# Seven loads of table rows issued as two DMAs each, by rows

## The chip, the cores and the metric

The kernel runs on one core of a Trainium2 chip (trn2). Its time is the device time of one execution, in microseconds (us); the figure for a kernel is the median of its runs. The profile is of one execution, by the hardware profiler, and its times count from the first instruction of the program. Engines: PE (matmuls), PEld (weight loads of PE), DVE (VectorE), ACT (ScalarE), POOL (GpSimd), SP (SyncE, which here only issues DMAs). A core has 16 DMA engines, and every DMA, whichever engine issues it, is carried out by some of these 16.

## The reference

The inputs are a list of 50 items for each of 1024 users, the lists' lengths, and a table of 100001 rows of 128 numbers (f32), whose row 0 counts as zero. What is computed, cut to the core:

```
e = emb[seq]                                  # 1024 x 50 x 128
uF = cumsum(e, axis=1) / min(t, lengths)      # running mean over the items
y = (uF - mean) * rsqrt(var + eps) * gamma + beta   # statistics over the 1024 users, for each t
v = v + (x - v) / 2; spike = v >= 1; v = v - spike  # scanned over the 50 steps
uF_out = mean of the spikes over the steps    # 1024 x 128
scores = uF_out @ emb.T                       # 1024 x 100001, f32
```

The output alone is 409.6 MB, and the table 51.2 MB.

## The kernel before, in words

**First stage** (to about 507 us, when the first store of scores is issued). For each of the 50 steps, rows of the table are gathered (POOL, L204, and 512 single-row DMAs on SP, L197), turned and summed on PE, normalised and compared on DVE and ACT, and spikes are counted. Meanwhile the first 36 blocks of the table (a block is 1024 rows) are loaded by SP into six tiles `rows0` to `rows5`.

**Second stage.** The table has 98 blocks `q`, the last one of 673 rows. A block lies in SBUF as 128 partitions of 1024 numbers, partition p holding rows 8p to 8p+7 of the block, 4 KB in one piece. Each block is prepared once: PE turns it (`turned`, L119), ACT copies the rounded part (`hi`, L141), DVE the rest (`lo`, L142). The 98 blocks are taken in 21 groups of `WIDTHS` blocks: first 2 or 3 at a time, then twelve groups of 6, then two of 4. For each group and each of the eight sets of 128 users (`n`), PE multiplies (`product`, L149) the counts with every block of the group, DVE and ACT in turn copy the result scaled by 1/50 into a tile `o` (L471, L473), and SP stores the tile (`store`, L158): 128 partitions of 24 KB where the group has 6 blocks, 3 MB a store. In the wide groups there are three tiles `o`, used in turn, so the copies for a store wait until the store three places back has landed.

**The loads of the change.** In the wide groups the remaining 62 blocks are loaded while the stores run: after `n` = 1 and `n` = 4 of a group, `fetch` is called for half a group, three blocks. Its DMA (L97) has 128 partitions, three blocks, and 4 KB in each, 1.5 MB, and is issued by ACT, in ACT's program order between its copies, since SP's queue is that of the stores. There are 20 such loads (q = 36, 39, ... 93); then one of a single block (q = 96) and two for the last block: 640 rows as 128 partitions of five pieces of 512 bytes (L106), and 33 rows as 33 partitions of 512 bytes (L111).

**What sets the order.** The order is written out by hand (`manual_schedule`): each engine does its instructions in the order in which the program records them. The completions of the DMAs of SP and ACT are counted by eight semaphores, DMAHW0 to DMAHW7, given out in turn, in program order, to stores and loads alike. A DMA that takes a semaphore waits on its issuing engine until the DMA eight places back, which had the same semaphore, has landed, unless that engine has waited for that already. A store on SP may so wait for a load of ACT.

Of the kernel before, what the change touches and what calls it, by code (L numbers as in the profile page):

```python
# [20 lines left out]
P = 128  # L21
BN_EPS = 1e-5
V_TH = 1.0
HALF = 1024
KQ = HALF // P
# [3 lines left out]

WIDTHS = [2, 2, 2, 3, 3, 3, 3] + 12 * [6] + [4, 4]  # L30
NARROW, MIDDLE = 3, 7


@with_exitstack
def rec_kernel(
# [44 lines left out]
    def size(q):  # L80
        return min(HALF, N - q * HALF)

    def group(g):
        at = g if g < AHEAD else AHEAD - 2 + g % 2
        r = rowp.tile([P, GROUP, HALF], F32, tag=f"rows{at}", name=f"rows_{g}")
        for k in range(GROUP):
            rows[g * GROUP + k] = r[:, k, :]
        return r

    def fetch(r, q, n):  # L90

        engine = nc.sync if q < AHEAD * GROUP else nc.scalar
        k = q % GROUP
        n = min(n, parts - q)
        whole = n - (size(q + n - 1) < HALF)
        if whole:
            engine.dma_start(  # L97
                out=r[:, k : k + whole, :],
                in_=table[q * HALF : (q + whole) * HALF, :].rearrange("(q p k) d -> p q (k d)", p=P, k=KQ),
            )  # L100
        if whole < n:
            full, rest = divmod(size(parts - 1), P)
            c1 = (parts - 1) * HALF
            r = r[:, k + whole, :].rearrange("p (k d) -> p k d", d=D)
            if full:
                engine.dma_start(  # L106
                    out=r[:, :full, :],
                    in_=table[c1 : c1 + full * P, :].rearrange("(k p) d -> p k d", p=P),
                )
            if rest:  # L110
                engine.dma_start(out=r[:rest, full, :], in_=table[c1 + full * P : N, :])  # L111
# [49 lines left out]
    with ExitStack() as ph:  # L161
# [17 lines left out]
        for g in range(AHEAD):  # L179
            fetch(group(g), g * GROUP, GROUP)  # L180
# [113 lines left out]
        whole = slice(0, B)  # L294
# [5 lines left out]
        for t in range(T):  # L300
# [35 lines left out]
            r = sp.tile([P, 1], F32, tag="r", name=f"r_{t}")  # L336
# [10 lines left out]
            q = sp.tile([P, 1], F32, tag="q", name=f"q_{t}")  # L347
# [13 lines left out]
            if not last:  # L361
# [9 lines left out]
                if t in (T - 8, T - 6):  # L371
                    q = (t - T + 8) // 2
# [54 lines left out]
    for c, W in enumerate(WIDTHS):  # L427
# [30 lines left out]
        for n in range(NB):  # L458
# [26 lines left out]
            if n in (1, 4) and c >= MIDDLE and to_fetch < parts:  # L485
                g = to_fetch // GROUP
                if to_fetch % GROUP or to_split >= (g - 1) * GROUP:
                    if to_fetch % GROUP == 0:
                        r = group(g)
                    fetch(r, to_fetch, GROUP // 2)  # L490
                    to_fetch += GROUP // 2
# [21 lines left out]
```

## Time and profile before

| what | value |
|---|---|
| median of 3 runs | 1779.58 us |
| lowest and highest | 1778.25 and 1783.5 us |
| span of the profiled execution, first to last instruction | 1569.9 us |
| the profiled execution's own time | not told by the page |
| median less span (work around the program) | 209.7 us |
| first store of scores issued, last one issued | 506.8 us, 1557.7 us |
| first and last of the three-block loads issued by ACT | 751.7 us, 1383.9 us |
| DMA engines, mean busy share, 700 to 1425 us | 1.00, at 424 GB/s |
| PE, DVE, ACT busy, 700 to 1425 us | 604, 388, 324 of 725 us |

The busy share of the DMA engines is a mean over 16, so it does not tell one engine from another. Two other records of the trace do. Each DMA engine that carries a part of a DMA adds one mark to the DMA's semaphore when its own part has landed, so a store has sixteen marks with a time each, and the store counts as landed at the sixteenth. And every packet that a DMA engine moves has a start, a duration, a size and a queue (q1 for SP's DMAs, q10 for ACT's), though no engine number.

### The profile page before, as it was taken

What the parts mean: (1) busy time and instruction counts of PE and PEld (TensorE: products, weight loads), DVE (VectorE), ACT (ScalarE), POOL (GpSimd) and SP (SyncE); (2) the same over time, 40 slices, a digit from 0 to 9 for tenths busy, and PEclk for the clock granted to TensorE, in tenths of its full rate; (3) what the DMA queues carried; (4) which work ended last, traced back from release to release, by engine and by line L of the source; (5) the groups of instructions that cost most, each with busy time, mean ns of one, the idle gap of its engine ahead of it and who ended that gap; (6) DMA issues with size and microseconds to landing.
All of it is one profiled execution on the core that took longest, in us unless ns stands there. A gap on an engine that the chain in (4) does not pass through costs nothing.

```text
span 1569.9 us, 14231 instructions
## 1 busy us (share of the span) xinstructions
PE 1153.1 (73%) x4548; PEld 822.3 (52%) x4548; DVE 940.7 (60%) x1161; ACT 630.6 (40%) x700; POOL 374.6 (24%) x402
## 2 busy tenths in 40 slices
PE   4555555555556988899878788887788888788784
PEld 2222222222233766677666666666666666666563
DVE  4777777777778665576545555555555545555453
ACT  2322222222233554465444444444444444444342
POOL 6777777777775000000000000000000000000000
PEclk7555555555555999999999988999999998989998
DMA  9622222222222999999999999999999999999998
GB/s 342 245 55 53 55 54 54 54 53 54 52 53 64 399 411 420 420 393 428 425 432 427 429 428 424 418 422 424 428 413 420 415 424 429 421 423 409 394 423 354
DMA packets 54600, 488.25 MB, mean 311 GB/s; under 512 B 12443, under 2 KB 13756, under 8 KB 33276
## 3 DMA queue, kind: packets, MB, share of 16 engines
q1 hardware_dynamic: 33008, 429.03, 65.1%
q0 software_dynamic: 12672, 25.98, 6.2%
q10 hardware_dynamic: 8844, 32.33, 5.2%
q8 instruction: 36, 0.59, 0.1%
q14 instruction: 40, 0.33, 0.1%
HBM read 77.69 MB, written 409.60 MB: 310 GB/s over the span
## 4 chain that ended last, share of the span: by engine, by line
DMA 52%; POOL 17%; PE 11%; issue 9%; ACT 5%; DVE 4%; DVEq 0%; ACTq 0%; SPq 0%; POOLq 0%
DMA scores<-o 49%; POOL e L204 17%; PE po L149 9%; ACT o L473 5%; DMA e<-in_L_rec_emb_table,idx 3%; DVE o L471 2%; PE pt L119 1%; DVE bs L323 1%; DVE uF L322 0%; DVE s L343 0%; PE pre L313 0%; PE sums L281 0%; DMA idx<-in_r_seq 0%; ACT hi L141 0%; ACT pairs L141 0%
## 5 line engine op out<-in xcount | busy, mean ns | idle before, releaser
L471 DVE TENSOR_SCALAR o<-po 128x1024 f32<-128x1024 f32 x391 | 463.5, 1220 | 351.8 <-DMA scores<-o 323.4
L473 ACT ACTIVATE o<-po 128x1024 f32<-128x1024 f32 (+1 forms) x391 | 387.9, 1018 | 547.8 <-DMA scores<-o 344.9
L204 POOL DMA_INDIRECT e<-in_L_rec_emb_table,idx x396 | 373.9, 944 | 123.4 <-issue 114.6
L149 PE MATMUL po<-pairs,countB 128*128 128x512 f32 x1168 | 314.7, 415 | 67.6 <-ACT o L473 50.7
L149 PEld LDWEIGHTS po<-pairs,countB 128*128 128x128 f32 x1168 | 225.8, 198 | 132.5 <-ACT o L473 65.8
L149 PE MATMUL po<-pairs,countC 128*128 128x512 f32 x876 | 239.1, 419 | 43.6 <-ACT o L473 43.6
L313 PE MATMUL pre<-ident,e 128*128 128x128 f32 x396 | 153.1, 450 | 143.8 <-DMA e<-in_L_rec_emb_table,idx 142.2
L149 PEld LDWEIGHTS po<-pairs,countC 128*128 128x128 f32 x876 | 170.1, 200 | 89.7 <-ACT o L473 54.7
L313 PEld LDWEIGHTS pre<-ident,e 128*128 128x128 f32 x396 | 78.5, 201 | 236.1 <-DMA e<-in_L_rec_emb_table,idx 214.7
L142 DVE TENSOR_TENSOR pairs<-pt,pairs 128x1024 fp32r<-128x1024 f32 (+1 forms) x73 | 88.3, 1217 | 96.6 <-ACT pairs L141 96.5
L337 ACT ACTIVATE r<-mv,eps 128x1 f32<-128x1 f32 x50 | 14.7, 295 | 300.6 <-DVE mv L333 300.6
L322 DVE SCALAR_TENSOR_TENSOR uF<-rlen,pre 128x512 f32<-128x512 f32 x100 | 68.3, 683 | 103.8 <-PE pre L313 103.8
L119 PE MATMUL pt<-ident,rows 128*128 128x128 f32 x782 | 113.5, 293 | 8.0 <-ACT o L473 3.9
L119 PEld LDWEIGHTS pt<-ident,rows 128*128 128x128 f32 x782 | 102.6, 154 | 28.8 <-issue 10.0
L149 PE MATMUL po<-hi,countB 128*128 128x512 f32 x200 | 82.8, 414 | 18.8 <-ACT o L473 13.8
L281 PE MATMUL sums<-s,ident_h 128*128 128x512 bf16 x98 | 49.6, 608 | 60.6 <-DVE s L343 60.6
L270 PE MATMUL pre<-zT,l 128*128 128x512 f32 x100 | 78.0, 782 | 21.6 <-DVE uF L322 21.5
L149 PE MATMUL po<-lo,countB 128*128 128x512 f32 x200 | 80.4, 402 | 0.0
L141 ACT CAST pairs<-pt 128x1024 fp32r<-128x1024 f32 (+1 forms) x73 | 73.6, 1008 | 16.2 <-PE pt L119 15.9
L149 PE MATMUL po<-pairs,countA 128*128 128x512 f32 (+1 forms) x292 | 73.2, 393 | 9.1 <-ACT o L473 9.1
L149 PE MATMUL po<-hi,countC 128*128 128x512 f32 x150 | 62.7, 418 | 16.4 <-ACT o L473 16.4
L356 ACT ACTIVATE v<-uF,hgb,a 128x1024 f32<-128x1024 f32 x49 | 59.2, 1208 | 37.4 <-DVE a L352 37.4
(78 smaller groups left out, 821.1 us busy)
## 6 DMA issues: line engine op xcount, KB each, us to landing
scores<-o SPq DMA_DIRECT2D x96, 3072.0 KB
scores<-o SPq DMA_DIRECT2D x32, 1536.0 KB
rows<-in_L_rec_emb_table ACTq DMA_DIRECT2D x20, 1536.0 KB
scores<-o SPq DMA_DIRECT2D x22, 1024.0 KB
rows<-in_L_rec_emb_table SPq DMA_DIRECT2D x6, 3072.0 KB
scores<-o SPq DMA_DIRECT2D x8, 2048.0 KB
scores<-o SPq DMA_DIRECT2D x8, 1872.5 KB
aside<-in_L_rec_emb_table SPq DMA_DIRECT2D x512, 0.5 KB
```

The costliest lines, as they stand in the source:

```text
L119: nc.tensor.transpose(pt[:, k0 : k0 + kw], r[:kw, k0 : k0 + D], ident[:kw, :kw])
L141: nc.scalar.copy(vh, vp)
L142: nc.vector.tensor_tensor(vl, vp, vh.bitcast(F32), ALU.subtract)
L149: nc.tensor.matmul(po[:, :kw], lhsT=counts[n], rhs=part[:, k0 : k0 + kw], start=j == 0, stop=j == 1,)
L204: nc.gpsimd.indirect_dma_start(out=es[t][:, n * P : (n + 1) * P], out_offset=None, in_=table, in_offset=bass.IndirectOffsetOnAxis(ap=idx[: ...
L270: nc.tensor.matmul(pre[h], lhsT=l, rhs=zT[:, h * BANK : (h + 1) * BANK], start=t == 0, stop=False, skip_group_check=True,)
L281: nc.tensor.matmul(sums[h], lhsT=ident_h, rhs=s[:, h * BANK : (h + 1) * BANK], start=t == 0, stop=t == T - 2, skip_group_check=True,)
L313: nc.tensor.matmul(pre[h][:, k : k + P], lhsT=aside[t] if h == k == 0 and t in aside else e[:, h * BANK + k : h * BANK + k + P], rhs=ident ...
L322: nc.vector.scalar_tensor_tensor(uF[:, cs], rlen[:, cs], 1.0 / (t + 1), pre[h], ALU.max, ALU.mult)
L356: nc.scalar.activation(vt, uF[:, cs], AF.Identity, bias=hgb[:, 1:2], scale=a)
L471: nc.vector.tensor_scalar_mul(o[:, h0 : h0 + hw], po[:, :hw], 1.0 / T)
L473: nc.scalar.mul(o[:, h0 : h0 + hw], po[:, :hw], 1.0 / T)
```

## The change

A table `CUTS` names seven of the 20 loads by their first block and gives a number of rows (partitions). Such a load is issued as two DMAs one right after the other, both by ACT into the same tile: the first has that number of partitions, the second has those left, all three blocks in both. All other loads stay as they were, and so does every other instruction. The bytes moved are the same.

```
+CUTS = {39: 120, 48: 126, 57: 104, 66: 108, 75: 88, 84: 120, 90: 120}
...
         if whole:
-            engine.dma_start(
-                out=r[:, k : k + whole, :],
-                in_=table[q * HALF : (q + whole) * HALF, :].rearrange("(q p k) d -> p q (k d)", p=P, k=KQ),
-            )
+            to = r[:, k : k + whole, :]
+            of = table[q * HALF : (q + whole) * HALF, :].rearrange("(q p k) d -> p q (k d)", p=P, k=KQ)
+            cut = CUTS.get(q, P)
+            engine.dma_start(out=to[:cut], in_=of[:cut])
+            if cut < P:
+                engine.dma_start(out=to[cut:], in_=of[cut:])
```

The second pieces have 8, 2, 24, 20, 40, 8 and 8 rows. As the semaphores are given out in turn, each added DMA moves all later DMAs one semaphore on. ACT has seven more instructions; four of them (q = 48, 66, 84, 90) begin with a wait for a semaphore that an earlier load has.

## The prediction

> **What bounds the kernel now.** I read the page first, for where the time lies, then the sums by stretch, the chain and SP's waits, and last the single packets and completion marks.
>
> The page, with the chain that ended last and two groups:
>
> ```profile
> span 1569.9 us, 14231 instructions
> ...
> q1 hardware_dynamic: 33008, 429.03, 65.1%
> ...
> q10 hardware_dynamic: 8844, 32.33, 5.2%
> ...
> DMA 52%; POOL 17%; PE 11%; issue 9%; ACT 5%; DVE 4%; DVEq 0%; ACTq 0%; SPq 0%; POOLq 0%
> ...
> L471 DVE TENSOR_SCALAR o<-po 128x1024 f32<-128x1024 f32 x391 | 463.5, 1220 | 351.8 <-DMA scores<-o 323.4
> L473 ACT ACTIVATE o<-po 128x1024 f32<-128x1024 f32 (+1 forms) x391 | 387.9, 1018 | 547.8 <-DMA scores<-o 344.9
> ```
>
> Stores carry half the chain, and both copying engines stand idle for them. The sums by stretch (us; busy times with counts; granted clock, DMA share, GB/s):
>
> ```profile
> 750.00:1000.00 250.00, 208.32 (x904) 164.39 (x902) 130.90 (x111) 109.96 (x112) 0.00 (x0) 0.92 1.01 426
> 1000.00:1425.00 425.00, 350.13 (x1506) 275.47 (x1507) 225.36 (x191) 186.83 (x190) 0.00 (x0) 0.93 1.00 421
> 1425.00:1475.00 50.00, 42.88 (x191) 33.56 (x190) 26.30 (x23) 22.45 (x23) 0.00 (x0) 0.97 0.95 394
> 1475.00:1563.00 88.00, 63.75 (x272) 49.31 (x270) 42.24 (x38) 32.48 (x36) 0.00 (x0) 0.95 1.00 422
> 1563.00:1570.00 7.00, 0.00 (x0) 0.00 (x0) 0.00 (x0) 0.00 (x0) 0.00 (x0) 0.50 0.08 34
> ```
>
> The DMA engines are full. Summing the packets, the mean engine idles 2.0 us from 750 to 1425, 3.1 us to 1475, 0.1 us to 1563 and 6.2 us after. So the question is not the mean, but which engine ends last. The chain's end (start, us, what):
>
> ```profile
> 1529.53 11.77 DMA scores<-o
> 1541.30 0.03 issue
> ...
> 1542.56 1.23 DVE o L471
> 1543.79 0.02 SPq L158
> 1543.81 0.03 issue
> 1543.84 11.33 DMA scores<-o
> ```
>
> A store takes 11.3 us to its last mark, though the last store's marks come at 1563.5 (the first), 1565.1, 1565.6 and 1568.8: one engine is 5.3 us behind the first. Packets tell which kind of engine. On one engine each packet starts 3 to 4 ns before the last one's end, so they can be threaded into sixteen sequences. Fifteen move a 24 KB store packet in 912 ns (median); one, which I call L, takes 931 to 936. It lags 2 us at 716, 8 us at 925, 7 to 10 us until 1420, and in the stretches that I threaded (1006 to 1563) it has no gap that is more than a packet. L's load packets (4 KB) take 163 ns in the mean, the others' 159. Three other engines lag 2 to 5 us.
>
> **How rows fall to engines.** A DMA of 128 rows leaves 16 marks, 8 rows to an engine; the one of 33 rows leaves 11, three rows each; the single-row ones use one engine. Each is the largest number up to 16 that divides the rows. So I take 120 rows on 15 engines, 126 on 14, 104 on 13, 108 on 12, 88 on 11, and second pieces of 8, 2, 24, 20, 40 rows on 8, 2, 12, 10, 10. If smaller sets lie inside larger ones, the seven loads give the engine in place 0, 1, ... 15: 70, 70, 69 (six times), 66, 66, 60, 52, 41, 33, 24 and 0 rows; before, each has 7 x 8 = 56.
>
> L has a place: it is among the eleven of the 33-row load. Its store packet of 1470.861 is followed at 1471.794 by a 512-byte q10 packet, after it had closed the 640-row load at 1470.855; L alone still had a store then. So L is in places 0 to 10, and gets 4 to 14 rows more.
>
> **The change part by part.**
> 1. *L's rows.* Eight of the eleven places get 13 or 14 rows, so I take 13. A row is three packets: 13 x 3 x 0.163 = 6.4 us; ends 4 x 3 x 0.163 = 2.0 and 14 x 3 x 0.163 = 6.8. Nothing hides it: L has no gap, and the copies wait for L's mark. **+6.4 us.**
> 2. *Relief of places 11 to 15* (4 to 56 rows less, up to 27 us at 0.159 a packet): these engines do not end last, and the stores wait for all sixteen. 0 here; rival A says when not.
> 3. *Seven more issues on ACT.* Rows:
>
> ```profile
> L97 ACTq DMA_DIRECT2D rows<-in_L_rec_emb_table x21: 347/375/417, 751.7 to 1424.9; - x21
> L106 ACTq DMA_DIRECT2D rows<-in_L_rec_emb_table x1: 1272/1272/1272, 1425.3 to 1425.3; - x1
> L111 ACTq DMA_DIRECT2D rows<-in_L_rec_emb_table x1: 1705/1705/1705, 1426.6 to 1426.6; - x1
> ```
>
>    Between 7 x 0.375 = 2.6 and 7 x 1.7 = 12 us of ACT, at seven places. The copies (L473) and the PE products behind them come that much later once, and SP's store with them. ACT idles 272 us for stores from 750 on, and L has a backlog of about 8 us, against 1.7 at most. 0; without that cover, up to 12.
> 4. *Four new waits on ACT* (second pieces of q = 48, 66, 84, 90, each for the load before). Those landed 12.5, 10.5, 8.6 and 9.1 us before the issue times of before. 0. Behind such a wait stand ACT's copies and SP's stores.
> 5. *Semaphores one on.* Stores now wait for loads one store sooner: ten such waits shrink from 11 to 15 us of margin to 2.2 to 8.0 (load 3.7, 2.8, 3.2, 2.2 us for q = 39, 48, 57, 66). Still margins: 0, and L's backlog is behind it. Rival B prices the other case.
> 6. *Later landing of the second pieces*: 40 rows on ten engines are 12 more packets, between store packets of 0.912: 12 x 1.07 = 13 us. PE turns a block 42 to 48 us after its load has landed. 0.
>
> The unchanged tail keeps its own stall, SP's wait for the 640-row load:
>
> ```profile
> SPq L158 <- DMA rows<-in_L_rec_emb_table: 13.9, 1, 13.9
> ```
>
> Sum: +6.4, so a span of 1576.3 and, against the median, 1779.6 + 6.4 = **1786.0 us**. The page doesn't tell the profiled execution's own time; I take the 209.7 us around the span as unchanged.
>
> [...] The trace has L in the eleven, which speaks against the change. No trace here shows engine numbers.
>
> **The rivals.**
> - *A, the relieved engines are the ones that bind (faster).* If the sets do not nest and L is outside most of them, L loses up to 56 rows and stops binding. Then the ten or so loaded engines bind: they ended 5.3 us earlier, had about 2 us of gaps, and get 6.2 us (13 x 3 x 0.159): -1. At best all gaps but the 3.1 us of the tail's stall go: -8. Middle -4: 1775.6. For: the relief is steep, and two of the three smaller laggards are outside the eleven. Against: L's packets at 1471. It decides as soon as L carries under 56 rows.
> - *B, a wait opens.* If load marks come 8 us later (L's backlog), the ten margins turn into about 33 us of waiting on SP. The 13.9 us of the tail cost the mean engine 3.1 us; at that rate 33 cost 7.4: 1786.0 + 7.4 = 1793.4. Decides when a load lands over 3 us later.
> - *C, packets of narrower DMAs are slower.* The gathers' 4 KB packets average 244 ns. L's 207 load packets at 244 instead of 163: +16.8, so 1802.8. Against: the 33-row load's packets took 27 ns like the 640-row load's.
> - *D, hidden.* L sits at place 10, or gains from emptier neighbours (its store packets take 912 at best): +1, 1780.6.
>
> **How the numbers follow.** Chances: forecast 0.50, A 0.26, D 0.12, B 0.08, C 0.04. 0.3% is 5.3 us, about what a measurement of this kernel can tell from no change. Faster is half of A: 0.13. Slower is 0.38 of the forecast's 0.50 (the rest has L at place 8 to 10) with B and C: 0.50. Same is 0.37. The forecast's own range is 1781.6 (+2.0) to 1787.5 (+6.8 and 1 us of scatter). For 8 in 10, half of A is left out below 1775.5 (0.13), C and part of B above 1793.5 (0.07).
>
> **What would show it.** Right: the sixteen marks of stores after 1290 spread over 10 us; the last store's last mark 5 or more us after the others; the mean engine's gaps from 750 to 1425 grow from 2.0 to about 8 us; first pieces leave 15, 14, 13, 12, 11 marks; SP waits for loads still in the tail alone. Wrong: a smaller spread of marks (A), new SP or ACT waits on loads (B), load packets over 170 ns (C).

## The result, and the profile after

The changed kernel takes 1786.09 us (median of 20 runs, 1781.49 to 1790.72); the kernel before, in the runs beside it, 1782.09 us (20 runs, 1774.44 to 1789.48). The ratio is 1.0023 with a 95% interval of 1.0012 to 1.0035, which is 4.0 us slower, between 2.1 and 6.2. That is smaller than the 0.3% that the prediction took as its bound. On a chip where the runs of the kernel before lie within 0.1% of each other, it was 5.9 us (the run `e_after` below); one slow run of 2154 us there is left out.

The page of the changed kernel (lines of the code have moved by four):

```profile
span 1786.1 us, 14228 instructions
...
q1 hardware_dynamic: 33008, 429.03, 57.2%
...
q10 hardware_dynamic: 8885, 32.33, 4.8%
...
DMA 43%; SPq 10%; PE 9%; issue 7%; ACT 5%; DVE 4%; DVEq 0%; ACTq 0%; another core or an unknown queue 0%
...
L475 DVE TENSOR_SCALAR o<-po 128x1024 f32<-128x1024 f32 x391 | 464.4, 1220 | 356.5 <-DMA scores<-o 310.8
L477 ACT ACTIVATE o<-po 128x1024 f32<-128x1024 f32 (+1 forms) x391 | 388.4, 1018 | 554.7 <-DMA scores<-o 333.7
```

The span is 216 us longer than that of the profile before, and almost all of it has nothing to do with the change. This execution's own time was 1787.85 us, so there are only 1.75 us around its span; the time lies inside, in the first stage. The single-row loads of SP there, first in the profile before, then in the one after (durations in ns, minimum/median/maximum; first and last start in us):

```profile
L197 SPq DMA_DIRECT2D aside<-in_L_rec_emb_table x512: 224/225/7507, 38.0 to 356.3; - x171
```

```profile
L201 SPq DMA_DIRECT2D aside<-in_L_rec_emb_table x512: 2/225/7463, 38.0 to 662.4; - x171
```

The same 512 DMAs are spread over 318 us in one execution and over 624 us in the other, and the first store of scores is issued at 506.8 and at 715.7 us. It is not the change that does this: on the chip of `e_after` the changed kernel's first store is at 506.5 us, and the kernel before has run in 1571 us there and in 1774 to 1789 us here. So the two profiles are compared from the first store on. By that the second stage takes 1063.1 us before and 1070.4 us after: 7.3 us more, of which 1.1 had arisen before the first divided load.

The sums by stretch, 209 us later than the stretches of the prediction, with the same columns (the last stretch is 6 us longer):

```profile
959.00:1209.00 250.00, 207.65 (x894) 163.40 (x894) 132.25 (x112) 110.27 (x112) 0.00 (x0) 0.92 1.00 424
1209.00:1634.00 425.00, 346.01 (x1496) 270.39 (x1495) 222.24 (x188) 185.22 (x188) 0.00 (x0) 0.94 1.00 418
1634.00:1684.00 50.00, 42.64 (x191) 33.48 (x189) 26.03 (x22) 22.30 (x23) 0.00 (x0) 0.97 0.99 413
1684.00:1778.00 94.00, 70.30 (x294) 54.69 (x294) 45.82 (x41) 35.44 (x39) 0.00 (x0) 0.93 0.96 404
```

The DMA engines are as full as before, but in the long stretch they move 418 GB/s where it was 421, and the copies done in it are 188 and 188 in place of 191 and 190. The chain still ends in stores and the copies that wait for them (start, us, what):

```profile
1745.72 11.77 DMA scores<-o
1757.71 1.05 issue
1758.76 1.22 DVE o L475
1760.03 11.34 DMA scores<-o
1771.50 1.22 DVE o L475
```

SP's wait for loads is one, as before, the tail's:

```profile
SPq L162 <- DMA rows<-in_L_rec_emb_table: 13.4, 1, 13.4
```

ACT's issues, the first pieces and whole loads (L102), and the seven second pieces (L104):

```profile
L102 ACTq DMA_DIRECT2D rows<-in_L_rec_emb_table x21: 322/396/602, 961.6 to 1641.2; - x21
L104 ACTq DMA_DIRECT2D rows<-in_L_rec_emb_table x7: 734/1303/1491, 988.4 to 1573.6; - x7
```

Each of the seven that come right behind another cost ACT 1.3 us in the median and not 0.4, 8.5 us in all.

### The profile page after: what moved, and what is told of

The parts are those of the page before. It is cut to its first block, busy times and chain, and to the rows that moved or that the text cites. A ratio compares the mean times of both kernels' runs of the same rounds, so it can differ in the third digit from the quotient of the medians.

```text
span 1786.1 us, 14228 instructions
## 1 busy us (share of the span) xinstructions
PE 1111.9 (62%) x4538; PEld 831.8 (47%) x4548; DVE 940.8 (53%) x1161; ACT 631.4 (35%) x700; POOL 374.5 (21%) x402
## 4 chain that ended last, share of the span: by engine, by line
DMA 43%; SPq 10%; PE 9%; issue 7%; ACT 5%; DVE 4%; DVEq 0%; ACTq 0%; another core or an unknown queue 0%
DMA scores<-o 43%; PE po L153 8%; SPq L201 8%; ACT o L477 4%; SPq L193 3%; DVE o L475 2%; DVE bs L327 0%; DVE uF L326 0%; DVE v L363 0%; ACT pairs L145 0%; DVE negv L369 0%; DVE s L347 0%; PE pt L123 0%; DVE pairs L146 0%; PE sums L153 0%
## 5 line engine op out<-in xcount | busy, mean ns | idle before, releaser
L274 PE MATMUL pre<-zT,l 128*128 128x512 f32 x100 | 74.2, 744 | 267.2 <-DVE uF L326 204.2
L274 PEld LDWEIGHTS pre<-zT,l 128*128 128x128 f32 x100 | 27.6, 277 | 308.0 <-issue 210.6
L317 PE MATMUL pre<-ident,e 128*128 128x128 f32 x396 | 98.5, 419 | 12.2 <-DMA e<-in_L_rec_emb_table,idx 7.5
L317 PEld LDWEIGHTS pre<-ident,e 128*128 128x128 f32 x396 | 85.1, 225 | 37.0 <-issue 25.3
L285 PE MATMUL sums<-s,ident_h 128*128 128x512 bf16 x88 | 45.3, 606 | 62.7 <-issue 52.0
L145 ACT CAST pairs<-pt 128x1024 fp32r<-128x1024 f32 (+1 forms) x73 | 73.6, 1008 | 13.7 <-PE pt L123 13.5
```

What stands on the lines that cost most here:

```text
L145: nc.scalar.copy(vh, vp)
L274: nc.tensor.matmul(pre[h], lhsT=l, rhs=zT[:, h * BANK : (h + 1) * BANK], start=t == 0, stop=False, skip_group_check=True,)
L317: nc.tensor.matmul(pre[h][:, k : k + P], lhsT=aside[t] if h == k == 0 and t in aside else e[:, h * BANK + k : h * BANK + k + P], rhs=ident ...
```

## The experiments

All kernels keep the computation whole. From here on "before" is the kernel before on the same chip as the experiment. Ten experiments were made: the first four on one chip, the next four on another (the kernel before takes 1571.4 and 1571.3 us there), the last two on one with the long first stage. Apart from `e_before` and `e_after` they replace the body of the load by a loop over a table of pieces:

```
-            cut = CUTS.get(q, P)
-            engine.dma_start(out=to[:cut], in_=of[:cut])
-            if cut < P:
-                engine.dma_start(out=to[cut:], in_=of[cut:])
+            at = 0
+            for rows_n in PIECES.get(q, [P]):
+                engine.dma_start(out=to[at : at + rows_n], in_=of[at : at + rows_n])
+                at += rows_n
```

**The kernel before once more (`e_before`), for its own time and the scatter of the second stage.**

> The kernel before once more, for the scatter of one profile. The second stage is taken from the issue of the first store to the end of the span: 1063.1 us in the profile of before, 1070.4 us after. If the change's rows are the cause, this run gives 1063 within 2 us, with one slow engine lagging up to 10 us and 5 us at the end. If the 7 us were chance between two executions, it may as well give 1067 or more. The first stage, 506.8 us to the first store in the one profile and 715.7 us in the other, may be either; it does not touch the second.

It took 1571.55 us with a span of 1569.8 us. The second stage is 1063.4 us, 0.3 us from that of the profile before, and each store landed within 0.8 us of the same place in it. The second stage of one profile can thus be compared with that of another to about 1 us, and the time around the span is 1.75 us here too. So the runs of 1778 to 1784 us must, by subtraction, have had a first stage about 208 us longer than the profiled one.

**Seven loads as halves of 64 rows (`e_even`): the issues, waits and semaphores of the change without its unequal rows.**

```
-CUTS = {39: 120, 48: 126, 57: 104, 66: 108, 75: 88, 84: 120, 90: 120}
+PIECES = {q: [64, 64] for q in (39, 48, 57, 66, 75, 84, 90)}
```

> The same seven loads divided into 64 and 64 rows. Each half goes to 16 engines, 4 rows each, so no engine gets more or fewer rows than before, while the seven more issues, the second pieces' waits on ACT and the semaphores one place on are those of the change. Rows on the slow engine as the cause: no change of the second stage, 1063 to 1065 us, ratio of times 0.999 to 1.001. Issues, waits or semaphores as the cause: as the change, 1068 to 1072 us, ratio 1.002 to 1.004.

Measured: 1571.53 us (11 runs, 1571.2 to 1572.74) against 1571.4; ratio 1.0001, 0.9992 to 1.001. The second stage is 1063.4 us. SP's waits for loads are the tail's alone:

```profile
SPq L163 <- DMA rows<-in_L_rec_emb_table: 13.5, 1, 13.5
```

Dividing seven loads so that each engine, counted as in the prediction, keeps its eight rows cost nothing that could be measured here (0.1 us, -1.3 to +1.6): not the seven issues, not the waits behind them, not the shifted semaphores.

**The ways of dividing on fourteen loads in place of seven (`e_double`).** Each of the change's ways twice as often, so 26 rows more for the engine L (1 for 120+8 and 126+2, 2 for 104+24, 3 for 108+20, 4 for 88+40).

```
+PIECES = {36: [120, 8], 39: [120, 8], 45: [126, 2], 48: [126, 2], 54: [104, 24], 57: [104, 24], 63: [108, 20],
+          66: [108, 20], 72: [88, 40], 75: [88, 40], 81: [120, 8], 84: [120, 8], 87: [120, 8], 90: [120, 8]}
```

> The change's seven ways of dividing, each used on two loads instead of one: 14 loads (q = 36, 39, 45, 48, 54, 57, 63, 66, 72, 75, 81, 84, 87, 90). The engines in places 2 to 7 get 26 rows more than before, places 0 and 1 get 28. Rows on the slow engine: 26 x 3 x 0.163 = 12.7 us, a second stage of 1075 to 1078 us. If the engine's lag only fills a slack once, the second dose costs less than the first: 1071 to 1073 us.

Measured: 1583.07 us (5 runs, 1582.9 to 1583.43) against 1571.4, +11.7 us; ratio 1.0074, 1.006 to 1.0088. The second stage is 12.0 us longer, and the surplus grows with the loads that are divided (2.4 us at store 100, 7.2 at 117, 11.1 at 140, 11.9 at the end; single stores scatter by 1 to 2 us). Per row of L that is 11.7 / 26 = 0.45 us. SP also waits for loads outside the tail here:

```profile
SPq L163 <- DMA rows<-in_L_rec_emb_table: 70.1, 7, 13.5
```

That is 56 us more than before, so this run alone does not tell rows from waits; `e_low` below does, where 109 us of such waiting cost 0.7 us at most.

**Where L stands (`e_place`).** Seven loads as 112 + r + (16 - r) rows, r = 1 to 7. The middle piece then has r engines with a row each (with r = 1, three engines with one of the row's three packets each), and L's mark is among its marks or is not.

```
+PIECES = {39: [112, 1, 15], 48: [112, 2, 14], 57: [112, 3, 13], 66: [112, 4, 12], 75: [112, 5, 11], 84: [112, 6, 10], 90: [112, 7, 9]}
```

> Where the slow engine stands among the sixteen. The seven loads are divided into 112 rows (16 engines, 7 each) and two small pieces of r and 16 - r rows, r = 1 to 7 from the first load to the last, one row to an engine, on the first r and the first 16 - r places if sets nest. The marks of the small pieces tell whether the slow engine, whose mark comes 3 us or more after the others, is among them. At place 7 it is in none of the first small pieces (1 to 7 rows) and in all of the second ones, has 8 rows of each load as before, and the second stage stays at 1063 to 1066 us. At a place p below 7 it is also in the pieces of more than p rows.

The marks of three middle pieces (us), with the end of L's part of the neighbouring pieces, from threading the packets:

```
r = 4: 1108.7 1109.2 1111.6 1112.2                 L ends its part of the 112 rows at 1112.8, of the 12 rows at 1117.0
r = 5: 1198.4 1198.5 1198.6 1200.6 1210.4          last mark of the 112 rows at 1207.0; L ends its part of the 11 rows at 1213.7
r = 7: last of seven 1387.0                        L ends its part of the 112 rows at 1382.8, of the 9 rows at 1390.3
```

With five engines one mark is 10 us behind the others, where L's turn would come, and with four there is none: between L's two neighbouring parts no mark falls. With r = 2 and 3, L has no part either. So L is in the sets of five engines and more and in none of four and fewer: if the sets lie inside one another, its place is the fifth. The time, of one run, was 1573.1 us, and the second stage 1064.7 us, 1.6 us longer; L has 3 rows more here (9 for 8 with r = 5, 6 and 7, 8 with the others), which is 1.4 us at 0.45.

**The changed kernel where the first stage is short (`e_after`).**

> The changed kernel itself, on the chip of this study's other experiments, where the kernel before takes 1571.4 us. Theory (engine L, at the fifth place, gets 13 rows more and has no gap): by the prediction's price 13 x 0.49 = 6.4 us, by the doubled ways of dividing (26 rows, 11.7 us) half of it, 5.9 us; so 1577.3 to 1577.8 us, a second stage of 1069 to 1070 us, and a last store whose marks spread over about 5 us or more. Rival (the wait that opens): new waits of SP or ACT for loads before the tail, and 13 us, 1584 us. Rival (relief): under 1571.4 us.

Measured: 1577.2 us (5 runs, 1577.04 to 1577.73) against 1571.26, +5.9 us; ratio 1.0039, 1.0026 to 1.0053. The second stage is 1068.9 us, 5.8 us longer; SP waits for loads 13.5 us, in the tail alone. 5.9 / 13 is again 0.45 us a row.

**Ten loads as 112 + 12 + 4 rows (`e_low`), and the same ten as 112 + 11 + 5 (`e_five`).** Both have the same number of DMAs in the same places. Counted as in the prediction, in the first places 0 to 3 get a row more in each load and the fifth place the eight that it had; in the second, places 0 to 4 get a row more. What differs is one row in each load, moved from the twelfth place to the fifth.

```
+PIECES = {q: [112, 12, 4] for q in (39, 45, 51, 57, 63, 69, 75, 81, 87, 93)}     # e_low
+PIECES = {q: [112, 11, 5] for q in (39, 45, 51, 57, 63, 69, 75, 81, 87, 93)}     # e_five
```

> Ten loads as three DMAs of 112, 12 and 4 rows. Against the kernel before, the engines at places 0 to 3 get 1 row more in each of the ten loads (+10), places 4 to 11 as many as before, places 12 to 15 one row less. Theory (only L at the fifth place binds, and the four engines ahead of it have about 5 us of slack): 0 to +0.5 us, 1571.4 to 1571.9 us. Rival (any engine with more rows binds, or three issues in place of one cost something): +4.5 to +4.9 us, 1575.9 to 1576.3 us.

> The same ten loads as three DMAs of 112, 11 and 5 rows. Places 0 to 4 get 1 row more in each (+10), places 5 to 10 as many as before, places 11 to 15 one row less. Against the run with 112, 12 and 4 rows, the engine at the fifth place is the only one that gets more. Theory (L is there and binds): 10 x 0.45 to 0.49 = +4.5 to +4.9 us, 1575.9 to 1576.3 us. Rival (L elsewhere, or its rows hidden): the same time as the run with 112, 12 and 4 rows.

Measured: 1571.99 us for the first (11 runs, 1571.71 to 1572.12; ratio 1.0005, 0.9995 to 1.0014) and 1576.3 us for the second (6 runs, 1575.86 to 1577.67; ratio 1.0032, 1.002 to 1.0044), against 1571.26. Ten rows on four other engines and twenty DMAs more: 0.7 us. One row more in ten loads on the fifth engine: 4.3 us beyond that, 0.43 us a row. SP's waits for loads, in the first kernel and in the second (us in total, times, longest):

```profile
SPq L163 <- DMA rows<-in_L_rec_emb_table: 122.4, 11, 13.5
```

```profile
SPq L163 <- DMA rows<-in_L_rec_emb_table: 121.8, 11, 15.4
```

Three pieces to a load use up the eight semaphores sooner, and now stores do wait for loads on SP, 109 us more in all than before. The first kernel shows that this waiting is worth at most its 0.7 us (2.2 at the interval's end). That the DMA engines had work while SP stood is concluded from that time.

**Taking rows from L (`e_relief`, `e_relief6`, `e_relief10`).** In `e_place` a piece of four rows left four marks and L's was not among them. So, if the sets lie inside one another, a load as 112 + 4 + 4 + 4 + 4 rows gives the fifth place and those behind it 7 rows for 8, and the four places ahead of it 11 for 8. This was done on three loads, on six and on ten.

```
+PIECES = {q: [112, 4, 4, 4, 4] for q in (48, 66, 84)}                                # e_relief
+PIECES = {q: [112, 4, 4, 4, 4] for q in (39, 48, 57, 66, 75, 84)}                    # e_relief6
+PIECES = {q: [112, 4, 4, 4, 4] for q in (39, 45, 51, 57, 63, 69, 75, 81, 87, 93)}    # e_relief10
```

> Three loads (first blocks 48, 66 and 84) as five DMAs of 112, 4, 4, 4 and 4 rows. The fifth place, L, gets 7 rows for 8 in each (-3 in all), as places 5 to 15; places 0 to 3 get 11 for 8 (+9 in all, 9 x 0.48 = 4.3 us, inside the 5.3 us by which they end ahead of L). Theory: 3 x 0.45 to 0.49 = 1.4 us less, 1570.0 us, second stage 1062 us. Rival (the engines ahead of L then end last, or five issues one after the other cost something): no gain, 1571.4 us or more.

Three loads: 1570.42 us (11 runs, 1569.87 to 1571.07) against 1571.26, 0.8 us less; ratio 0.9995, 0.9986 to 1.0004, so a gain isn't established. The second stage is 0.9 us shorter. The direction is the expected one, the size 0.28 us for each of L's rows and not 0.45. SP's waits for loads are 47.1 us here, 33.6 more than the tail's in `e_before`.

> The five pieces of 112, 4, 4, 4 and 4 rows on six loads instead of three (first blocks 39, 48, 57, 66, 75, 84): the fifth place, L, -6 rows, places 0 to 3 +18 rows. Theory (what counts is L's rows): twice the measured gain of three loads, 0.84 us, so -1.7 us (at the full price of a row -2.7 us), 1568.6 to 1569.6 us. Rival (places 0 to 3 now end last: 18 x 0.45 = 8.1 us more for them against the 5.3 us that they had): their excess of 2.8 us and more, 1571.3 us or slower.

> The same five pieces on ten loads (first blocks 39, 45, ... 93): L -10 rows, places 0 to 3 +30 rows. Theory: -2.8 us at the measured price of three loads, -4.5 us at the full price of a row, 1566.8 to 1568.5 us. Rival (places 0 to 3 end last: 30 x 0.45 = 13.5 us more against 5.3 us): 8 us slower, about 1579 us. Between the two ends the time tells how much slack the engines ahead of L have over the whole stage.

These two ran on the chip with the long first stage. Six loads: 1777.39 us (12 runs) against 1779.41; ratio 0.9993, 0.9974 to 1.0012, which tells neither case from the other. The second stage of its profile speaks against a gain: 1063.9 us, 0.8 us longer than in the profile before, with 162.5 us of waits of SP for loads. Ten loads: 1789.41 us (8 runs) against 1779.41, +10.0 us; ratio 1.0056, 1.0032 to 1.008, and a second stage 8.0 us longer. One engine no longer stands far behind the others: the last store's marks come between 1784.6 and 1787.1 us, the last four at 1785.6, 1786.5, 1786.6 and 1787.1, where before one engine was 3.2 us behind the next. Which engines these four are, the marks do not tell. SP waited for loads far more,

```profile
SPq L163 <- DMA rows<-in_L_rec_emb_table: 317.3, 22, 18.0
```

but the size would fit the rows alone: 30 rows more on four engines at 0.45 us are 13.5 us, less the 5.3 us by which the first engines ended ahead of L, 8.2. How much of it the waits add was not taken apart, so what made this kernel slower is argued and not shown. No kernel was found that beats the one before by more than its measurement can tell.

## Why the prediction was right in sign and mechanism, point by point

The forecast was +6.4 us. Measured were +4.0 (2.1 to 6.2) in the result's runs, whose interval just leaves the forecast out, and +5.9 (4.1 to 8.3) in `e_after`, whose interval holds it. The forecast median of 1786.0 us lies on the measured 1786.09 partly by luck: the median of the kernel before was 2.5 us higher in the twenty runs than in the three that the forecast started from, and the difference is what the working was about.

- **One engine sets the pace.** Right, and now shown: the pair of 112 + 12 + 4 and 112 + 11 + 5 differs only in which engine gets a row, and its 4.3 us appear when that engine is the fifth.
- **How rows fall to engines.** Right. The first pieces left 15, 14, 13, 12 and 11 marks of engines that carried data and the second pieces 8, 2, 12, 10 and 10. (Each DMA on fewer than sixteen engines left one mark more, 0.5 to 2.2 us after its issue, long before its data.) That the sets lie inside one another fits L's marks in `e_place` and the times of the pair; engine by engine it was not shown. A load of a single row, in `e_place`, used three engines for its three packets, which the largest divisor of its rows, one, does not give.
- **L in the first eleven places, 13 rows more.** Right, though 13 was chosen as the commonest number of eleven places. The fifth place was only found by the experiments: by marks on one chip, and by the times of the pair on another. In the profile after, L is seen in the pieces on eight engines and more: in the last two pieces of eight rows one mark comes 4.2 and 5.2 us behind the other seven.
- **0.489 us a row.** Slightly large: 0.45 in the doubled run, 0.45 in `e_after`, 0.43 in the pair. The term was 6.4 and measured 5.9 us. It came from the mean duration of L's load packets, 163 ns. That is no sign that L is slow at loads: the 159 ns set beside it for the other engines can only be a median, since the mean of all 7808 load packets in that profile is 164.3 ns. That all of it would show in the time, since L has no gap, was the assumption. What takes the 8% off isn't settled, and the interval of the doubled run (9.4 to 13.8 us) would still hold the full price of 12.7.
- **Relief of places 11 to 15 worth nothing.** Right: no gain appeared, with up to 56 rows taken from them. Rival A failed with its condition, since L carried more than 56 rows.
- **Issues on ACT, its four waits, the ten shrunken margins, the later second pieces: 0.** Right in the sum of the first three: `e_even` has as many DMAs in the same places, and costs 0.1 us (-1.3 to +1.6). After the change SP waited for loads in the tail alone, and PE did not wait for a load.
- **Rival B** did not occur in the change, but the runs say that its price was wrong, and more so than the forecast. It took 33 us of SP's waiting to cost 7.4 us, from the tail's 13.9 us and the mean engine's 3.1 us of idling there. In `e_low` 109 us of such waiting, 24 us by that rate, cost 0.7. In the tail the mean engine idled 3.1 us, but L had no gap longer than a packet (931 to 936 ns) there.
- **Rival C** occurred in part and did not matter. The mean load packet went from 164 ns (both profiles of the kernel before) to 171 ns in both profiles of the changed one, over the prediction's own limit of 170; the median stayed at 159, and 304 to 365 packets of 7808 took over 250 ns where it was 95 to 124. `e_low` has 169 ns and cost 0.7 us, so this can't be much of the 5.9 us. The prediction's 244 ns for the gathers' 4 KB packets is 236 ns in the profile before, which makes the rival's price 15.1 us and not 16.8.
- **The signs.** Two of them were badly chosen. The mean engine's gaps in the stretch from 750 to 1425 us were to grow from 2.0 to 8 us; they are 2.3 us in the profile after (209 us later) and 3.5 us in `e_after`. From 750 us to the last store's issue, which came 5.5 us later in `e_after`, the mean engine idled 7.3 us in place of 5.2, and the longer load packets took (171.6 - 164.3) x 7808 / 16 = 3.6 us of each engine: together 5.7. So the others' spare time went into longer packets more than into gaps in this count. And the marks of the stores were to spread over more than 10 us: they did up to 12.0 us in the profile after, but most lie between 8 and 11, before between 7 and 10. In `e_double`, with twice the rows, they spread no further than 12.0 us either: the copies for the store three places on wait for L's mark, so what grows is the time and not the lag. The last store's 5.3 us are the same in both kernels and told nothing.
- **"I take the 209.7 us around the span as unchanged."** Wrong as a reading. There is 1.75 us around the span. The rest of the 209.7 us was, by subtraction, a longer first stage in the runs that were timed than in the one that was profiled; the profiles of long executions have it. It changed nothing in the difference, because the change lies in the second stage, but in a kernel with work moved between the stages the sum would have been made against the wrong one.

If the sets lie inside one another, the slow engine is the one in the fifth place; its 24 KB packets took 931 to 936 ns in the profile before, against a median of 912 on the others. No trace here shows engine numbers.

## What to carry to other kernels

Where all DMA engines are full, as here (a busy share of 1.00 at 418 to 424 GB/s), a transfer can cost by the rows that it puts on the slowest engine and not by its bytes: with the bytes unchanged, 13 rows more on L came with 5.9 us (`e_after`), and ten rows more on each of the four engines ahead of it with 0.7 us (`e_low`). With 30 rows more on each of those four the kernel took 10.0 us more (`e_relief10`), for which their rows are argued as the cause and not shown. So count for each engine what every DMA gives it. The pieces of the change left as many marks with data as the largest divisor of their rows up to 16: 15 for 120 rows, 11 for 88, 12 for 24, 2 for 2. Halves of 64 rows, a multiple of 16, cost 0.1 us (`e_even`, -1.3 to +1.6). Two kernels with the same DMAs that move one row from one engine to another tell which engine binds, at 0.43 us for 12 KB here. A wait on the queue that issues DMAs need not cost its length (109 us for 0.7 here); and before time is put outside a span, compare the stages of two executions.

## What was not expected of the hardware

- A single DMA engine about 2% slower than the rest (931 to 936 ns for a 24 KB packet, against 912) sets the pace of a stage of 1063 us: ten rows more on it took 4.3 us. The four engines ahead of it in the sets took 10 rows more each for 0.7 us.
- SP stood 109 us more for loads in `e_low`, spread over ten waits, and the kernel took 0.7 us longer.
- A DMA issued right behind another took ACT 1.3 us (median of seven), one alone 0.4 us. It was not so everywhere: on one load of `e_relief` four in a row took 0.4 to 0.5 us each.
- The first stage has two lengths, 507 us and 713 to 717 us to the first store, by the execution or the chip and not by the kernel, and the 512 single-row DMAs of SP then take 624 us in place of 318. Why was not tried.
- With divided loads more of the 7808 load packets of 4 KB take longer than 250 ns: 304 and 365 in the two profiles of the changed kernel, 124 and 95 before. Where dividing leaves the rows even it is 254 (`e_even`, at a mean of 167 ns); with pieces of four rows it is 83 in `e_relief` and 99 in `e_relief10`, but 248 in `e_relief6`. What slows them stays open.
